# Expert tiles of a graph network with routed experts: features turned by a transposing DMA instead of TensorE

## The chip, the cores and the metric

The kernel runs on one core of a Trainium2 chip. The metric is device time in microseconds (us) of one launch. A core has five engines that each work through their own queue in order: PE (TensorE, products and transposes by a matmul with an identity), ACT (ScalarE), DVE (VectorE), POOL (GpSimd) and SP (SyncE, here only an issuer of DMAs). DMAs are issued from SP, ACT or POOL and run on 16 shared DMA engines.

## The reference

Two layers over 3327 nodes with 256 features. Each has a graph attention and a per-node network. The stage that is changed is the mixture of experts of layer 0; the rest stays as it is.

```python
# layer 0
x = x + gat(layernorm(x), adj)                  # two heads
x = x + experts(layernorm(x))
# layer 1
x = x + gat1(layernorm(x), adj)                 # one head
x = x + recurrence(layernorm(x))                # 30 steps: tanh, silu, layernorm, 256x256 product

def experts(x):                                 # 16 experts, hidden size 512
    probs = softmax(x @ gate_w + gate_b)
    top_probs, top_idx = top_k(probs, 2)        # two experts a node, weights normalized
    hidden = silu(x @ w1[e]) * (x @ w2[e])      # for every expert e
    return sum over the two experts of weight * (hidden @ w3[e])
```

## The kernel before

Nodes lie in 26 tiles of 128 rows. The stages run one after the other: projections of layer 0, attention of layer 0, experts, projections and attention of layer 1, and the recurrence. While the attention's last row groups run, the router (`route`, L510) writes the normalized rows to DRAM (`table_x`) and puts every node's two choices into lists by expert (`list_tokens`, L591, scatters from POOL).

**Tiles of the experts.** `find_tiles` (L662) cuts the lists into tiles of 128 choices of one expert and gives each a slot. It runs twice: for slots 0 to 15 (`FIRST` = 16) from the first 16 node tiles, full tiles only, and for the slots from 16 on once all nodes are listed. There are 61 slots that are always worked (`ALWAYS`), and a conditional rest up to 67. For each slot it works out the expert (`table`), the rows to gather (`which`), the rows to scatter to (`to`) and the weights of the choices. `two[:, 0, :]` (L651) holds the tile numbers by slot: here tile k of the pass is in the k-th slot of the pass.

**Weights.** Three sets of expert matrices (w1, w2, w3, 512 KB each) are held, slot s using set s % 3 (`SETS`). `weights(s)` (L788) issues three loads on SP, under a condition from the third slot on (L796): `table[1, s]` is whether the expert of slot s differs from that of slot s-3 (L720), so a load is skipped when the set already holds the right expert.

**The loop.** `work_off` (L861) runs over the slots. In iteration s it issues on POOL the gather of slot s+4 (`gathered`, L757, an indirect DMA of 128 rows into a part of `rb`, two buffers of three slots each); on PE the product with w1 (`product`, L830, L835), on ACT its silu (L881), on PE the product with w2, on DVE the product of both (L885, `pT`); then the next slot's features are turned: two PE transposes with `ident` (L826) into PSUM and a copy on ACT to `hT` (L827) (`features_first`, L822); then `results(s-1)` (L846): the product with w3 on PE (L851), the weighting on DVE (L854), and the scatter from POOL to `given` (L855); last, `weights(s+2)` on SP. `e` and `pT` come from the pool `run` with three buffers of 768 columns, of which the experts use 512.

At s = 16 whatever is left of the second `find_tiles` is flushed, and `layer1_parameters` (L359) issues six loads from ACT's queue; at s = 22 `score_vectors` (L371) does four small products on DVE. A scheduler orders the instructions of each engine by priority and by dependence, unless the kernel pins them (`keep_in_program_order`, `issue_after`, manual dependences).

**The recurrence** at the end already turns four of its seven row groups by DMA: ACT copies the float32 values as two planes of int16 halves (L1095), SP writes them to DRAM (`apart`, L1097), and SP reads them back with a transposing DMA (L1107), two tiles of 128x256 at a time.

Of the kernel before, what the change touches and what calls it, by code (L numbers as in the profile page):

```python
# [21 lines left out]
P = 128  # L22
# [5 lines left out]
MOST = 6  # L28
# [3 lines left out]
def gat_moe_gat_recurrent_ffn(ctx: ExitStack, tc: tile.TileContext, a: dict, out: bass.AP):  # L32
    nc = tc.nc
    N, D = a["x"].shape
    KD = D // P
# [6 lines left out]
    HID = a["w1"].shape[2]  # L42
    FH = HID // P
# [54 lines left out]
    ident = const.tile([P, P], F32, name="ident")  # L98
# [260 lines left out]
    def layer1_parameters():  # L359
        for dst, src in (  # L360
            (wv1[:, :, 2:], a["gW"].rearrange("(k p) c -> p k c", p=P)),
            (va.rearrange("p s d -> p (s d)"), every_partition(a["ga"], 2 * D)),
            (fW, a["fWT"].rearrange("(k p) d -> p k d", p=P)),
            (lw, a["ln_w"]),
            (lb, a["ln_b"]),
            (fb, every_partition(a["fb"], D)),
        ):
            tc.keep_in_program_order(nc.scalar.dma_start(dst, src))
        nc.vector.memset(ones_r, 1.0)

    def score_vectors():  # L371
# [10 lines left out]
    with ExitStack() as moe:  # L382
# [22 lines left out]
        ps_o = moe.enter_context(tc.tile_pool(name="ps0o", bufs=2, space=PSUM))  # L405
# [5 lines left out]
        with ExitStack() as pre:  # L411
# [58 lines left out]
            behind = None  # L470
# [9 lines left out]
            for ts in groups0[1:3]:  # L480
                behind = take_graph(ts, behind)
# [23 lines left out]
        run = moe.enter_context(tc.tile_pool(name="edge0", bufs=3))  # L505
        rows_p = moe.enter_context(tc.tile_pool(name="rows0", bufs=2))
        gate = moe.enter_context(tc.tile_pool(name="gate", bufs=1))
        turn = moe.enter_context(tc.tile_pool(name="turn", bufs=2))

        def route(ts):  # L510

            n, t0 = len(ts), ts[0]
            whole = [P, n, E]
            normalized([x[:, t, :] for t in ts], [row[:, j, :] for j in range(n)])
            here = slice(t0 * P, (t0 + n) * P)
# [6 lines left out]
            for j0 in range(0, n, 2):  # L522
                hT = turned(row[:, j0 : j0 + 2, :], turn, ps)
# [16 lines left out]
            logit, one, two, tmp = gtile("logit"), gtile("one"), gtile("two"), gtile("tmp")  # L540
# [41 lines left out]
            d, both = gcol("d"), gcol("both")  # L582
# [28 lines left out]
            if ts is groups0[3]:  # L611

                for s in range(3):
                    ahead.append(gathered(s))
            if ts is groups0[2]:
                pieces = begin_tiles()

# [27 lines left out]
        row = gate.tile([P, MOST, D], F32, name="row")  # L645
# [16 lines left out]
        def find_tiles(end, s0, n):  # L662


            here = slice(s0, s0 + n)
# [53 lines left out]
            s1 = max(s0, SETS)  # L719
# [35 lines left out]
        places = []  # L755

        def gathered(s):  # L757
            if s % 3 == 0 or s == ALWAYS:
                places.append(rows_p.tile([P, MOST * P], F32, name="rb"))
            row = places[-1][:, (s % 3) * D : (s % 3 + 1) * D]  # L760
            nc.gpsimd.indirect_dma_start(  # L761
                out=row, out_offset=None, in_=table_x[: EARLY * P, :] if s < FIRST else table_x,
                in_offset=bass.IndirectOffsetOnAxis(ap=which[:, s : s + 1], axis=0),
            )
            return row

        behind = None
        sets = [first_set]
# [53 lines left out]
        def features_first(row):  # L822
            pt = ps_o.tile([P, 512], F32, name="acc0")[:, :D].rearrange("p (k q) -> p k q", k=KD)
            hT = turn.tile([P, 2, KD, P], F32, name="hT")[:, 0]
            for k in range(KD):
                nc.tensor.transpose(pt[:, k, :], row[:, k * P : (k + 1) * P], ident)  # L826
            nc.scalar.copy(hT, pt)  # L827
            return hT

        def product(hT, w):  # L830

            p = bank().rearrange("p (f q) -> p f q", f=FH)
            for f in range(FH):
                for k in range(KD):
                    nc.tensor.matmul(  # L835
                        p[:, f, :], lhsT=w[:, k, f * P : (f + 1) * P], rhs=hT[:, k, :],
                        start=(k == 0), stop=(k == KD - 1),
                    )
            return p

        def edge(name):
            return run.tile([P, MOST * P], F32, name=name)[:, :HID].rearrange("p (f q) -> p f q", f=FH)

        ahead = deque()

        def results(s, hidT):  # L846

            w3 = ew[s % SETS][2]
            po = ps_o.tile([P, 512], F32, name="acc1")[:, :D]
            for f in range(FH):  # L850
                nc.tensor.matmul(po, lhsT=hidT[:, f, :], rhs=w3[:, f, :], start=(f == 0), stop=(f == FH - 1))  # L851
            y0 = 6 * KD * HID + s % 2 * D
            y = sets[1][:, y0 : y0 + D]
            nc.vector.tensor_scalar(y, po, weight[:, s : s + 1], None, op0=ALU.mult)  # L854
            put = nc.gpsimd.indirect_dma_start(  # L855
                out=given, out_offset=bass.IndirectOffsetOnAxis(ap=to[:, s : s + 1], axis=0), in_=y, in_offset=None
            )
            tc.declare_no_dep(put.ins, group="given", reason="no two results have the same row")
            tc.add_to_no_dep_group("given", put.ins)

        def work_off(s0, s1, aside):  # L861

            hT = features_first(ahead.popleft())
            made = None
            for s in range(s0, s1 + 1):
                if s == FIRST:
                    for _ in aside:
                        pass
                    layer1_parameters()
                if s == FIRST + 6:  # L870
                    score_vectors()
                hidT = made
                if s == 1:

                    results(0, hidT)
                if s < s1:
                    if s + 4 < s1:
                        ahead.append(gathered(s + 4))
                    pa = product(hT, ew[s % SETS][0])
                    act = edge("e")  # L880
                    nc.scalar.activation(act, pa, AF.Silu)  # L881
                    next(aside, None)
                    pb = product(hT, ew[s % SETS][1])
                    made = edge("pT")
                    nc.vector.tensor_tensor(made, act, pb, ALU.mult)  # L885
                    if s + 1 < s1:
                        hT = features_first(ahead.popleft())
# [17 lines left out]
        ahead.append(gathered(3))  # L905
        weights(1)


# [23 lines left out]
        )  # L932
        behind = None
        with tc.If(more > ALWAYS - FIRST):
            ahead.extend(gathered(s) for s in range(ALWAYS, ALWAYS + 4))
# [14 lines left out]
    with ExitStack() as st:  # L950
# [6 lines left out]
        ps_o = st.enter_context(tc.tile_pool(name="ps2o", bufs=2, space=PSUM))  # L957
# [38 lines left out]
        run = st.enter_context(tc.tile_pool(name="edge2", bufs=3))  # L996
# [26 lines left out]
    with ExitStack() as st:  # L1023
        ps_t = st.enter_context(tc.tile_pool(name="ps3t", bufs=2, space=PSUM))
        turns = cycle((ps, ps_t))
        ps_o = st.enter_context(tc.tile_pool(name="ps3o", bufs=2, space=PSUM))
# [11 lines left out]
        class Group:  # L1038
# [8 lines left out]
            def put(self, ins):  # L1047
                return tc.keep_in_program_order(ins) if self.at >= COUNT else ins
# [164 lines left out]
```

## Time and profile before

| | |
|---|---|
| median of 3 runs | 1842.49 us (1841.95 to 1842.71) |
| the profiled execution | 1841.14 us, its span 1839.4 us |
| PE busy / PEld busy | 1787.4 us (97%) / 1631.7 us (89%) |
| DVE / ACT / POOL busy | 1319.1 us (72%) / 1223.9 us (67%) / 888.4 us (48%) |
| mean granted PE clock | 0.995 |
| experts: first product, last scatter issued | 388.4 us, 741.5 us |
| PE transposes of the stage (L826) | 122, in 61 tiles |
| evictions of them on ACT (L827) | 61, 372 ns each |
| loads of weights issued (L800 to L802) | 183, 512 KB each |
| DMA transposes of the recurrence (L1107) | 236, 1241 ns to issue |
| copies into two planes (L1095) | 236, 1045 ns each |

The profiled execution is one run of its own; its span runs from the first to the last instruction. In the views, PE is the matmul, PEld the loading of its stationary operand, which overlaps it, and SPq the queue of SP. A line such as `L826 PE MATMUL acc<-ident,rb` names the line of the code, the engine, the operation, the tile written and the tiles read. In a timeline the first number is the start and the second the length, both in us; consecutive instructions of a kind are merged, with their count at the end.

### The profile page before, as it was taken

How to read it: one execution, taken by the hardware profiler on the slowest of the kernel's cores; microseconds unless marked ns; L12 is line 12 of the kernel's file. 1: busy time of each engine (PE TensorE's matmuls, PEld its weight loads, DVE VectorE, ACT ScalarE, POOL GpSimd, SP SyncE). 2: the span in 40 equal slices, each digit the busy share in tenths (PEclk: the TensorE clock that was granted, in tenths of full speed). 3: DMA queues.
4: the chain of work that ended last, by engine and by line, in shares of the span. 5: the costliest groups of instructions: out<-in, count | busy, mean ns of one | idle time of the engine just before them, and what ended most of it. 6: DMA issues, size and time to landing. Idle time of an engine off the chain costs nothing.

```text
span 1839.4 us, 32502 instructions
## 1 busy us (share of the span) xinstructions
PE 1787.4 (97%) x10980; PEld 1631.7 (89%) x10980; DVE 1319.1 (72%) x4039; ACT 1223.9 (67%) x1587; POOL 888.4 (48%) x654
## 2 busy tenths in 40 slices
PE   7999999999999999799999999999999999999997
PEld 6999999898999999688888878888888888888886
DVE  6888878853222222657677678999999999999998
ACT  2877667642111111366666579999999999999994
POOL 3010212155333332100111028988898889888984
PEclk9999999999999999899999999999999999999999
DMA  8887360258999886400000036666667666666667
GB/s 178 114 123 91 66 101 16 67 187 255 349 345 333 304 301 225 159 9 22 14 18 22 12 84 172 172 172 168 171 167 178 173 172 172 172 167 169 175 172 218
DMA packets 458610, 284.44 MB, mean 155 GB/s; under 512 B 305269, under 2 KB 418220, under 8 KB 458442
## 3 DMA queue, kind: packets, MB, share of 16 engines
q1 hardware_dynamic: 442322, 249.47, 48.4%
q0 software_dynamic: 11440, 28.09, 8.8%
q10 hardware_dynamic: 4680, 4.76, 0.8%
q8 instruction: 90, 1.47, 0.3%
q14 instruction: 78, 0.64, 0.1%
HBM read 168.19 MB, written 91.69 MB: 141 GB/s over the span
## 4 chain that ended last, share of the span: by engine, by line
PE 67%; issue 10%; DVE 6%; POOL 5%; DMA 3%; ACT 1%; another core or an unknown queue 0%; SPq 0%; POOLq 0%; DVEq 0%; ACTq 0%
PE po L1120 35%; PE acc L286 24%; PE bank L1085 4%; DVE pT L281 3%; POOL given L855 2%; POOL rb L761 2%; DMA given<-wh,to 2%; PE bank L835 1%; PE acc L163 1%; PE bank L148 1%; DMA old<-kept 1%; PE bank L526 1%; PE acc L851 1%; DMA lists<-pair,ati 0%; DVE x L1130 0%
## 5 line engine op out<-in xcount | busy, mean ns | idle before, releaser
L276 ACT ACTIVATE e<-rb,minus,full 128x384 f32<-128x384 f32 (+3 forms) x494 | 399.2, 823 | 168.6 <-DVE pT L281 150.8
L1055 POOL TENSOR_TENSOR th<-th,x 128x1024 f32<-128x1024 f32 (+1 forms) x210 | 465.0, 2214 | 94.1 <-ACT th L1052 86.4
L281 DVE SCALAR_TENSOR_TENSOR pT<-e,part,adjT 128x384 f32<-128x384 f32 (+3 forms) x494 | 383.5, 782 | 117.8 <-PE acc L286 101.9
L1120 PE MATMUL po<-wc,adjT 128*128 128x256 f32 x1888 | 422.2, 379 | 0.0
L1120 PEld LDWEIGHTS po<-wc,adjT 128*128 128x128 f32 x1888 | 356.4, 190 | 47.6 <-DVE x L1130 0.3
L1130 DVE SCALAR_TENSOR_TENSOR x<-po,rr,bb 128x256 f32<-128x256 f32 x780 | 325.1, 478 | 61.8 <-PE po L1120 61.2
L286 PE MATMUL acc<-wh,pT 128*128 128x129 f32 x2704 | 311.0, 276 | 2.3 <-DVE pT L281 2.3
L286 PEld LDWEIGHTS acc<-wh,pT 128*128 128x128 f32 x2704 | 305.5, 192 | 3.6 <-DVE pT L281 3.0
L286 PE MATMUL acc<-s_wh,pT 128*128 128x257 f32 x1352 | 295.5, 381 | 3.6 <-DVE pT L281 3.6
L286 PEld LDWEIGHTS acc<-s_wh,pT 128*128 128x128 f32 x1352 | 255.8, 190 | 42.7 <-DVE pT L281 7.0
L1120 PE MATMUL po<-wc,zT 128*128 128x256 f32 x1232 | 281.0, 379 | 0.8 <-DVE x L1130 0.8
L1064 DVE BATCH_NORM_STATS2 stats<-z 128x6 f32<-128x256 f32 x780 | 274.1, 412 | 1.4 <-ACT z L1059 1.4
L1120 PEld LDWEIGHTS po<-wc,zT 128*128 128x128 f32 x1232 | 229.2, 190 | 29.7 <-issue 1.1
L1095 ACT COPY adjT<-z 128x1024 int16<-128x1024 int16 x236 | 235.2, 1044 | 4.8 <-DVE pT L281 2.0
L121 POOL TENSOR_TENSOR rstd<-ve,neg_half 128x4 f32<-128x4 f32 (+3 forms) x28 | 32.0, 1141 | 410.4 <-DVE ve L119 312.3
L1052 ACT ACTIVATE th<-x 128x1024 f32<-128x1024 f32 (+1 forms) x210 | 209.2, 996 | 29.0 <-DVE x L1130 23.8
L1075 POOL TENSOR_TENSOR rr<-rr,neg_half 128x4 f32<-128x4 f32 (+1 forms) x210 | 206.8, 985 | 26.4 <-DVE rr L1070 26.3
L1059 ACT ACTIVATE z<-th 128x1024 f32<-128x1024 f32 (+1 forms) x210 | 207.0, 986 | 7.9 <-POOL th L1055 1.8
L885 DVE TENSOR_TENSOR pT<-e,bank 128x512 f32<-128x512 f32 x61 | 41.9, 688 | 179.7 <-PE bank L835 119.6
L881 ACT ACTIVATE e<-bank 128x512 f32<-128x512 f32 x61 | 36.4, 597 | 196.9 <-PE bank L835 117.2
L835 PEld LDWEIGHTS bank<-hT,wh 128*128 128x128 f32 x1280 | 149.6, 192 | 9.3 <-issue 4.5
L835 PE MATMUL bank<-hT,wh 128*128 128x128 f32 x1280 | 150.6, 276 | 6.5 <-ACT hT L827 2.5
(196 smaller groups left out, 1546.6 us busy)
## 6 DMA issues: line engine op xcount, KB each, us to landing
wh<-in_w_dram SPq DMA_DIRECT2D x120, 512.0 KB
apart<-adjT SPq DMA_DIRECT2D x236, 256.0 KB
first_set<-in_w_dram SPq DMA_DIRECT2D x63, 512.0 KB
in_bytes<-in_adj_dram POOLq DMA_DIRECT2D x3, 2496.0 KB
adjT<-apart SPq DMA_TRANSPOSE x236
x<-in_x_dram SPq DMA_DIRECT2D x6, 512.0 KB
kept<-x SPq DMA_DIRECT2D x8, 384.0 KB
old<-kept SPq DMA_DIRECT2D x6, 512.0 KB
```

The source lines that it names most:

```text
L276: nc.scalar.activation(e[:, : n * P], rb[:, : n * P], AF.Relu, scale=sc.full[:, j, h : h + 1], bias=sc.minus[:, j, h : h + 1],)
L281: masked = nc.vector.scalar_tensor_tensor(pT[:, : n * P], e[:, : n * P], sc.part[:, j, h : h + 1], adjT[:, j // 2, ts[0] * P : (ts[-1] + 1 ...
L286: nc.tensor.matmul(po[c], lhsT=pT[:, c * P : (c + 1) * P], rhs=wh[:, j, h, :], start=(j == 0 and c % per_bank == 0), stop=(j == NT - 1), s ...
L835: nc.tensor.matmul(p[:, f, :], lhsT=w[:, k, f * P : (f + 1) * P], rhs=hT[:, k, :], start=(k == 0), stop=(k == KD - 1),)
L1052: self.put(nc.scalar.activation(self.th, self.hs, AF.Tanh, scale=1.0 / S))
L1055: self.put(nc.gpsimd.tensor_tensor(self.th, self.th, self.hs, ALU.add))
L1059: self.put(nc.scalar.activation(self.z, self.th, AF.Silu, scale=1.0 / S))
L1064: self.put(nc.vector.bn_stats(stats[:, j, :], self.z[:, j, :]))
L1075: self.put(nc.gpsimd.tensor_tensor(r, r, neg_half[:, : self.n], ALU.pow))
L1095: self.put(nc.scalar.copy(parts[:, c : c + 2], halves[:, c : c + 2]))
L1120: nc.tensor.matmul(self.po[:, j, :], lhsT=self.zT(j, k), rhs=wc[:, k, :], start=(k == 0), stop=(k == KD - 1),)
L1130: nc.vector.scalar_tensor_tensor(self.hs[:, j, :], self.po[:, j, :], self.r[:, j : j + 1], bb, op0=ALU.mult, op1=ALU.add)
```

## The change

From slot 19 (`FIRST + 3`) to slot 60 the features are no longer turned on PE. In iteration s:

- on ACT, behind the silu of slot s, the gathered rows of slot s+4 are copied as two planes of int16 halves into the 256 columns of the `e` tile that the experts don't use (`put`), and POOL writes them to DRAM (`asked`, six buffers);
- on SP, after the results of slot s-1 and ahead of `weights(s+2)`, a transposing DMA reads slot s+2 back into `face` (three buffers) (`face`);
- `features_first(s)` then only hands over the `face` tile.

Slots before 19, and the conditional ones after 60, are turned as before. From s = 17 on the gathers run five slots ahead instead of four (two of them are issued at s = 16). PE's products of these slots are tied into the order in which they are written. `layer1_parameters` issues one load per slot from s = 16 on, and `score_vectors` stands at s = 24.

The tile numbers of the slots are laid out anew: in each pass, the slots of one lane (every third slot, the ones that share a weight set) hold consecutive tiles, first all of lane 0, then lane 1, then lane 2.

```diff
@@ layer1_parameters
             tc.keep_in_program_order(nc.scalar.dma_start(dst, src))
+            yield
@@
+        faces = moe.enter_context(tc.tile_pool(name="faces", bufs=3))
@@ tile numbers of the slots
-        numbers(two[:, 0, :], [[1, SLOTS]], 0, 0)
+        for s0, n in ((0, FIRST), (FIRST, ALWAYS - FIRST)):
+            no = 0
+            for lane in range(SETS):
+                here = two[:, 0, s0 + lane : s0 + n : SETS]
+                numbers(here, [[1, here.shape[1]]], no, 0)
+                no += here.shape[1]
+        numbers(two[:, 0, ALWAYS:], [[1, SLOTS - ALWAYS]], ALWAYS - FIRST, 0)
@@ find_tiles
-            tile_no = two[:, 0, :n]
+            tile_no = two[:, 0, here]
@@
+        def by_dma(s):
+            return FIRST + 3 <= s < ALWAYS
...
+        def put(s, room, behind):
+            planes = room.bitcast(I16)
+            with tc.issue_after(behind):
+                nc.scalar.copy(
+                    planes.rearrange("p (b d) -> p b d", b=2),
+                    gotten.pop(s).bitcast(I16).rearrange("p (d b) -> p b d", b=2),
+                )
+            put_down[s] = next(asked)
+            nc.gpsimd.dma_start(put_down[s], planes)
+
+        def face(s):
+            faces_of[s] = faces.tile([P, KD, P], F32, name="face")
+            nc.sync.dma_start(
+                faces_of[s].bitcast(I16), put_down.pop(s).rearrange("t (b d) -> (t b) d", b=2), transpose=True
+            )
+
+        def features_first(s):
+            if by_dma(s):
+                return faces_of.pop(s)
+            row = gotten.pop(s)
...
@@ work_off
+            parameters = layer1_parameters()
...
+                tied = by_dma(s)
                 if s == FIRST:
                     for _ in aside:
                         pass
-                    layer1_parameters()
-                if s == FIRST + 6:
+                if s == FIRST + 8:
                     score_vectors()
...
-                    if s + 4 < s1:
-                        ahead.append(gathered(s + 4))
+                    for q in range(s + 4 if s <= FIRST else s + 5, min(s + (5 if s < FIRST else 6), s1)):
+                        gathered(q)
                     pa = product(hT, ew[s % SETS][0])
-                    act = edge("e")
-                    nc.scalar.activation(act, pa, AF.Silu)
+                    act, room = edge("e")
+                    silu = nc.scalar.activation(act, pa, AF.Silu).ins
+                    if by_dma(s + 4):
+                        put(s + 4, room[:, HID : HID + D], silu)
+                    if FIRST <= s < ALWAYS:
+                        next(parameters, None)
                     next(aside, None)
...
                 if s > max(s0, 1):
                     results(s - 1, hidT)
+                if by_dma(s + 2):
+                    face(s + 2)
                 if s + SETS - 1 < s1:
                     weights(s + SETS - 1)
```

More of the change, by code (lines that the diff above doesn't have):

```diff
@@ L613, in route @@
                 for s in range(3):
-                    ahead.append(gathered(s))
+                    gathered(s)
             if ts is groups0[2]:
@@ L753, in find_tiles @@
             nc.vector.tensor_tensor(to[:, here], tof, spare, ALU.add)
-        places = []
+        places, asked = [], cycle([dram.tile([P, 2 * D], I16, name=f"asked{q}") for q in range(6)])
+        gotten, put_down, faces_of = {}, {}, {}
+        def by_dma(s):
+            return FIRST + 3 <= s < ALWAYS
         def gathered(s):
@@ L759, in gathered @@
                 places.append(rows_p.tile([P, MOST * P], F32, name="rb"))
-            row = places[-1][:, (s % 3) * D : (s % 3 + 1) * D]
+            rows = places[-1][:, (s % 3) * D : (s % 3 + 1) * D]
             nc.gpsimd.indirect_dma_start(
-                out=row, out_offset=None, in_=table_x[: EARLY * P, :] if s < FIRST else table_x,
+                out=rows, out_offset=None, in_=table_x[: EARLY * P, :] if s < FIRST else table_x,
                 in_offset=bass.IndirectOffsetOnAxis(ap=which[:, s : s + 1], axis=0),
             )
-            return row
+            gotten[s] = rows
+        def put(s, room, behind):
[16 more added lines that the diff above has]
+            row = gotten.pop(s)
+            pt = ps_o.tile([P, 512], F32, name="acc0")[:, :D].rearrange("p (k q) -> p k q", k=KD)
+            hT = turn.tile([P, 2, KD, P], F32, name="hT")[:, 0]
+            for k in range(KD):
+                nc.tensor.transpose(pt[:, k, :], row[:, k * P : (k + 1) * P], ident)
+            nc.scalar.copy(hT, pt)
+            return hT
         behind = None
@@ L820, in recurrence_parameters, with behind_latest @@
                 nc.vector.tensor_scalar(wc[:, k, :], wc[:, k, :], S, None, op0=ALU.mult)
[L822 to L828, printed above, removed]
+        tied, latest = False, None
+        def behind_latest(ins):
+            nonlocal latest
+            if tied and latest:
+                tc.add_manual_dep(
+                    ins.ins, latest.name,
+                    mybir.DependencyInfo(mybir.DependencyClass.NoSync, mybir.DependencyReason.DATA),
+                    reason="the experts' products in their order",
+                )
+            latest = ins.ins
         def product(hT, w):
@@ L834, in product @@
                 for k in range(KD):
-                    nc.tensor.matmul(
-                        p[:, f, :], lhsT=w[:, k, f * P : (f + 1) * P], rhs=hT[:, k, :],
-                        start=(k == 0), stop=(k == KD - 1),
+                    behind_latest(
+                        nc.tensor.matmul(
+                            p[:, f, :], lhsT=w[:, k, f * P : (f + 1) * P], rhs=hT[:, k, :],
+                            start=(k == 0), stop=(k == KD - 1),
+                        )
                     )
@@ L841, in edge @@
         def edge(name):
-            return run.tile([P, MOST * P], F32, name=name)[:, :HID].rearrange("p (f q) -> p f q", f=FH)
-        ahead = deque()
+            room = run.tile([P, MOST * P], F32, name=name)
+            return room[:, :HID].rearrange("p (f q) -> p f q", f=FH), room
         def results(s, hidT):
@@ L850, in results @@
             for f in range(FH):
-                nc.tensor.matmul(po, lhsT=hidT[:, f, :], rhs=w3[:, f, :], start=(f == 0), stop=(f == FH - 1))
+                behind_latest(
+                    nc.tensor.matmul(po, lhsT=hidT[:, f, :], rhs=w3[:, f, :], start=(f == 0), stop=(f == FH - 1))
+                )
             y0 = 6 * KD * HID + s % 2 * D
@@ L861, in work_off @@
         def work_off(s0, s1, aside):
-            hT = features_first(ahead.popleft())
+            nonlocal tied
+            parameters = layer1_parameters()
+            hT = features_first(s0)
             made = None
             for s in range(s0, s1 + 1):
+                tied = by_dma(s)
                 if s == FIRST:
@@ L876, in work_off @@
                 if s < s1:
-                    if s + 4 < s1:
-                        ahead.append(gathered(s + 4))
+                    for q in range(s + 4 if s <= FIRST else s + 5, min(s + (5 if s < FIRST else 6), s1)):
+                        gathered(q)
                     pa = product(hT, ew[s % SETS][0])
-                    act = edge("e")
-                    nc.scalar.activation(act, pa, AF.Silu)
+                    act, room = edge("e")
[4 more added lines that the diff above has]
+                        next(parameters, None)
                     next(aside, None)
                     pb = product(hT, ew[s % SETS][1])
-                    made = edge("pT")
+                    made, _ = edge("pT")
                     nc.vector.tensor_tensor(made, act, pb, ALU.mult)
                     if s + 1 < s1:
-                        hT = features_first(ahead.popleft())
+                        hT = features_first(s + 1)
                 if s > max(s0, 1):
                     results(s - 1, hidT)
+                if by_dma(s + 2):
+                    face(s + 2)
                 if s + SETS - 1 < s1:
@@ L904, in gat_moe_gat_recurrent_ffn @@
         )
-        ahead.append(gathered(3))
+        gathered(3)
         weights(1)
@@ L934, in gat_moe_gat_recurrent_ffn @@
         with tc.If(more > ALWAYS - FIRST):
-            ahead.extend(gathered(s) for s in range(ALWAYS, ALWAYS + 4))
+            for s in range(ALWAYS, ALWAYS + 5):
+                gathered(s)
             for s in range(ALWAYS, ALWAYS + SETS - 1):
```

## Prediction

> **What bounds the kernel now.** I read the page's 40 slices first (which stage is it, and what is full there), then the window table of that stage, then the timeline of a single expert tile, and last the waits of the DMA queue. Slices 9 to 16 are the expert stage (about 388 to 741 us):
>
> ```profile
> PE   7999999999999999799999999999999999999997
> ...
> DMA  8887360258999886400000036666667666666667
> ```
>
> PE and DMA are both full there, so the first question is which of them sets the pace. The window table (us, then busy time of PE, PEld, DVE, ACT, POOL, clock, DMA share, GB/s):
>
> ```profile
> 540.00:560.00 20.00, 20.00 (x157) 19.33 (x156) 4.00 (x7) 3.50 (x7) 6.82 (x7) 1.00 0.95 332
> 640.00:660.00 20.00, 20.00 (x159) 19.38 (x158) 3.90 (x7) 3.50 (x7) 6.83 (x7) 1.00 0.85 275
> 700.00:720.00 20.00, 20.00 (x157) 19.33 (x156) 4.26 (x8) 3.50 (x7) 4.89 (x5) 1.00 0.78 252
> ```
>
> The DMA share falls from 0.95 to 0.78 and PE does the same work in the same time. A stage that DMA paced would have sped up. One tile, and then the last tile, in the timeline:
>
> ```profile
> 562.22 3.76 PEld L835 LDWEIGHTS bank<-hT,wh 128*128 128x128 f32 x32
> 565.90 0.25 PEld L826 LDWEIGHTS acc<-ident,rb 128*128 128x128 f32 x2
> 566.12 1.60 PEld L851 LDWEIGHTS acc<-wh,pT 128*128 128x128 f32 x8
> 567.74 3.76 PEld L835 LDWEIGHTS bank<-hT,first_set 128*128 128x128 f32 x32
> ...
> 733.29 3.76 PEld L835 LDWEIGHTS bank<-hT,first_set 128*128 128x128 f32 x32
> 736.97 1.60 PEld L851 LDWEIGHTS acc<-wh,pT 128*128 128x128 f32 x8
> ```
>
> Differences of starts give the prices: products 565.90-562.22 = 3.68, the two transposes 0.22, the results 1.62, together 5.52 us, and no gap. (733.29-567.74)/30 = 5.518 confirms it over 30 tiles. Tile 60 has no successor to transpose, and its results start 3.68 after its products: without transposes the 0.22 is simply gone. The waits of SP say who waits for whom:
>
> ```profile
> SPq L802 <- PE acc L851: 120.9, 52, 5.3
> ```
>
> Weight loads wait for PE (a set is free only after its results), not PE for weights. PE is the bound, at 5.52 us a tile.
>
> [...]The trace has 273 ns as a record's length, but a step of 0.11 us per transpose, since records overlap; I use 0.11. [...]The last scatter (issued 741.50) releases its reader at 747.14, so up to 5.6 us here.
>
> **The change part by part.** Tiles 19 to 60 (42 of 61) lose the PE transposes. Write s for the tile whose products run.
>
> *Removed from PE:* 42 x 0.22 = 9.2 us, all of it on the path, for PE is gapless from 460 to 741 and what follows waits for the last scatter.
>
> *ACT:* a copy of 128x512 int16 (the same copy of 128x1024 takes 1.045 us at L1095, so about 0.53) replaces the eviction of 0.37. ACT is busy 3.5 of 20 us. The copy for s+4 stands behind silu(s) and waits for gather s+4; behind it on ACT is silu(s+1), due one tile later, and DVE's product needs that at the end of s+1. Cover about 3 us; beyond it the products' PSUM banks would come free late.
>
> *POOL:* one plain DMA per tile more. Not shown in this stage; from 0.57 to 0.94 us at L424, 0.97 for an indirect one. I take 0.97: 3 a tile, 2.9 plus 0.3 between each, in 5.3 us. The put waits for the ACT copy; queued behind it are the scatter of s-1 and the next gathers. The scatter has two result buffers, 10.6 us. Gathers come in threes when the last of an older three has been read; now they wait for copies four tiles ahead, instead of the transposes (40.7 us of POOL waits), so they move earlier.
>
> *SP:* one transposing DMA per tile, of half the size of L1107's: 0.62 to 1.24 us, I take 1.24. It waits for the put and for the third-last face to be used; behind it are the loads for s+2. Put(q) is issued about 3.4 us into tile q-4 and landed, with the slow 5.6, at 9; face(q) comes after the results of q-4, about 10.6 us after q-4 began, [...]with 5.6, 17.5; PE wants it at 4 x 5.3 = 21.2. [...]if the cover goes, each us late is a PE us per tile. Taken value 0, bounds 0 and +0.2 a tile (8 us); it cannot be a gain.
>
> *DMA engines.* In the last stage 236 pairs of put and transposed read (two tiles each) run in 730 us at a share of 0.67: 730 x 0.67/236 = 2.07, or 1.04 us a tile. From 470 to 735 us (48 tiles):
>
> ```profile
> q1 hardware_dynamic: 46703, 68.30, 75.8%
> q0 software_dynamic: 4387, 11.96, 12.7%
> ```
>
> 0.758 x 5.52 = 4.18 us of weights, 0.70 of gather and scatter. Added to 1.04 this is 5.92, more than a tile of 5.30. But the diff also renumbers the tiles: find_tiles' table now runs through every third slot, so one expert's tiles share a weight set and a load is skipped when the expert stays (the condition of L796). Counting the reference's routing with L662's rules: today 38 of the slots from 19 on load (slots 44, 51, 55, 59 skip; the trace has exactly four L802 issues under 0.1 us there, at 639.89, 678.52, 700.59, 722.66), afterwards 16 do. A load costs about 4.18 x 48/44 = 4.6 us, so 16/42 x 4.6 + 0.70 + 1.04 = 3.5 us of 5.30. DMA goes to a share near 0.65 and is no bound.
>
> *Before tile 19:* of slots 0 to 15, 11 load instead of 16. PE has two stalls there, 2.3 us at 435.6 with no releaser shown and 1.7 at 455.6 for a weight load. Slots 6 and 7, around the first, now skip; slot 10, the second, still loads, behind the list read of L667. Bounds -4.0 to +2 (reordering); I take -1.0.
>
> *Handover (15 to 21):* put(19) and put(20) are issued in the iteration of their own gather. The trace has gathers 18 to 20 at 478.38 to 481.9, and put(19) can't come before silu(15) at 487.2: 5 us. Gather 21 waits for the transposes of tile 17 (494.9), put(21) for silu(17) near 498.5: 3.6 us. Taken 0; upper bound one late gather, 5 us.
>
> *Moved or tied, at nothing:* parameters one per tile (ACT's six issues cost 489.2 to 492.9 in a stage where PE showed no gap); score vectors two tiles later (4 x 0.43 us of DVE, which is idle 15 of 20 us); six more IOTAs at about 20.4 us (0.2 each, before 2.5 us of POOL idleness at 21 to 23.5); the order of products is the one PE already has. The tail is unchanged.
>
> Sum against the profiled execution: 1841.1 - 9.2 - 1.0 = 1830.9 (span 1829.2). The median of the runs is 1.35 above that execution, so 1832.2.
>
> **The rivals.**
> A, *gone stalls*: both early stalls vanish with the skipped loads: 1842.5 - 9.2 - 4.0 = 1829.3. For it: fewer loads in flight. Against: the second is a queue order that remains. 0.12.
> B, *handover or late faces eat it*: 3 to 8 us given back around tiles 15 to 21 or at 0.1 to 0.2 a tile, 1835.2 to 1840.2. For it: the copies wait on gathers on an in-order engine. Against: the spare times above. 0.15.
> C, *slower, DMA becomes the bound*: if skipped loads don't take effect, a tile needs 5.92 us of DMA: 42 x (5.92-5.52) = +17, 1859. It decides from 4.6 n/42 + 1.74 = 5.52, n = 35 loads on: more than 35 of 42 is slower. For it: share 0.95 today. Against: the count of 16 and the four skips that fit. The same sign comes if the transposing reads hold up the weight packets behind them in SP's queue. 0.10.
> D, *the change doesn't do what it says*: faces are made but PE's order leaves a gap as long as the transposes, 1842. 0.05.
>
> **How the numbers follow.** Forecast 0.58, from 1830 to 1835. Under 1828 about 0.05, over 1838 about 0.15; range 1828 to 1838. What a measurement can tell from no change is about 0.2%, 3.7 us. Faster than 1838.8: 0.58 + 0.12 + 0.11 of B = 0.81; same: D and the rest of B, 0.09; slower: C, 0.10.
>
> **What would show it.** Right: L826 falls from 122 to 38 transposes; starts of L851 in steady tiles lie 5.30 apart; PE stays at 20.00 of 20 from tile 22 on; DMA share 0.5 to 0.7; some 42 transposing issues more on SP, 1.2 us each or less; L802 issues under 0.1 us become frequent. Wrong: PE waits on "face" (B, or late faces), DMA share near 1 and PE waits on weights (C), ACT idle for a gather ahead of the copy, or a step other than 5.30 with no wait shown. The forecast fails if the round trip over copy, put and read takes longer than four tiles.

## The result, and the profile after

The changed kernel takes 1834.82 us (median of 6 runs, 1833.87 to 1836.06); beside it the kernel before took 1842.48 us (6 runs, 1839.82 to 1843.16). The ratio is 0.9960, with a 95% interval of 0.9949 to 0.9970: 7.7 us faster, between 5.5 and 9.4. The forecast was 1832.2, range 1828 to 1838. The sign and the size hold; 2.6 us of the forecast gain are missing, and the experiments ask where they went. The profiled execution took 1833.87 us, its span 1832.1 (1839.4 before).

The slices of the page, in the same order as before:

```profile
PE   7999999999999999899999999999999999999998
...
DMA  8897360257696885400000037777777777777777
```

In the middle of the expert stage (slices 10 to 15) the DMA digits 8 9 9 9 8 8 of before are 7 6 9 6 8 8 now, and PE is full as before. The window table has the same columns (stretch; its length, then busy time of PE, PEld, DVE, ACT and POOL; clock; DMA share; GB/s):

```profile
540.00:560.00 20.00, 20.00 (x151) 19.17 (x151) 4.33 (x8) 4.42 (x8) 9.70 (x13) 1.00 0.60 139
640.00:660.00 20.00, 20.00 (x154) 19.25 (x153) 3.44 (x7) 4.42 (x8) 10.82 (x13) 1.00 0.81 249
700.00:720.00 20.00, 20.00 (x152) 19.17 (x151) 4.68 (x8) 3.07 (x6) 4.34 (x6) 1.00 0.84 216
```

PE is still the bound. POOL has one DMA more per tile (L788, 575 ns) and ACT's copy is longer than the eviction was (L783, 611 ns, against 372); neither is near full, POOL at 4.3 to 10.8 of 20 us and ACT at 3.1 to 4.4. In PEld's timeline a tile now has two kinds of work instead of three:

```profile
559.37 3.76 PEld L880 LDWEIGHTS bank<-face,wh 128*128 128x128 f32 x32
563.04 1.60 PEld L897 LDWEIGHTS acc<-wh,pT 128*128 128x128 f32 x8
564.67 3.42 PEld L880 LDWEIGHTS bank<-face,first_set 128*128 128x128 f32 x29
...
723.92 3.76 PEld L880 LDWEIGHTS bank<-face,first_set 128*128 128x128 f32 x32
727.60 1.60 PEld L897 LDWEIGHTS acc<-wh,pT 128*128 128x128 f32 x8
729.22 1.70 PEld L897 LDWEIGHTS acc<-first_set,pT 128*128 128x128 f32 x8
```

The products of tile 60, the last, start at 723.92 and those of the tile 30 before it at 564.67: (723.92-564.67)/30 = 5.308 us a tile, where it was 5.518. No gap stands in brackets, and no wait of PE names `face`. SP's waits show that the loads still wait for PE, as before, only in fewer cases, and that the new reads hardly wait for their puts:

```profile
SPq L842 <- PE acc L897: 64.1, 36, 5.4
...
SPq L792 <- DMA asked<-e: 0.9, 1, 0.9
```

From 470 to 735 us the queues carry:

```profile
q1 hardware_dynamic: 44288, 36.97, 49.2%
q0 software_dynamic: 6525, 17.83, 26.7%
```

q1, which holds the weights and the transposing reads, falls from 75.8 to 49.2%; q0, with gathers, puts and scatters, rises from 12.7 to 26.7%. Of the 45 issues of L842 from 484 us on, 26 took less than 0.1 us, the skipped ones; of L802's 45 before it was 4. (A skipped load leaves a record too, so the count of 183 issues stays as it was.)

**Where the 7.3 us between the two profiles came from.** The starts of PE's instructions cut each span into stages. Times in us; the last three columns are profiles of the experiments below.

| stage | before | after | e9, before again | e6, changed again | e10, none by DMA |
|---|---|---|---|---|---|
| to the first product of the experts | 388.6 | 388.4 | 389.0 | 386.4 | 386.8 |
| to the results of slot 12 | 89.3 | 89.1 | 88.4 | 87.7 | 89.0 |
| to the last result (slots 13 to 60) | 262.4 | 253.4 | 262.4 | 253.4 | 262.3 |
| to the first transposes of layer 1 (L148) | 12.3 | 13.3 | 13.0 | 12.5 | 12.6 |
| to the recurrence's first product | 338.5 | 341.0 | 340.7 | 341.4 | 338.8 |
| recurrence, to its last product | 739.2 | 738.9 | 739.0 | 738.5 | 744.5 |
| to the end | 9.1 | 8.0 | 8.5 | 8.2 | 8.5 |
| span | 1839.4 | 1832.1 | 1841.0 | 1828.1 | 1842.5 |

The stage that was changed gains 9.0 us in both profiles. 1.0 us goes before layer 1, and 2.5 us in layer 1's attention, in which no instruction was changed. There the clock shows a difference, in a stretch that PE fills either way. After:

```profile
782.00:786.00 4.00, 4.00 (x13) 3.19 (x12) 1.31 (x3) 2.54 (x5) 0.00 (x0) 0.57 0.19 49
```

and the same work before:

```profile
790.00:794.00 4.00, 4.00 (x20) 3.51 (x19) 2.11 (x4) 2.85 (x5) 0.00 (x0) 1.00 0.15 49
```

In four full us PE did 13 matmuls at a clock of 0.57, against 20 at 1.00.

### The profile page after: what moved, and what is told of

The parts are those of the page before. It is cut to its first block, busy times and chain, and to the rows that moved or that the text cites. A ratio compares the mean times of both kernels' runs of the same rounds, so it can differ in the third digit from the quotient of the medians.

```text
span 1832.1 us, 32461 instructions
## 1 busy us (share of the span) xinstructions
PE 1781.9 (97%) x10896; PEld 1626.0 (89%) x10896; DVE 1318.7 (72%) x4039; ACT 1229.3 (67%) x1587; POOL 914.2 (50%) x702
## 4 chain that ended last, share of the span: by engine, by line
PE 55%; DVE 3%; DMA 1%; issue 0%; ACT 0%; SPq 0%; POOL 0%; ACTq 0%; DVEq 0%; POOLq 0%
PE po L1176 35%; PE acc L286 15%; PE bank L1141 4%; PE acc L163 1%; DVE pT L281 1%; DMA old<-kept 0%; DVE x L1186 0%; DMA given<-wh,to 0%; PE bank L148 0%; DVE stats L1120 0%; DVE x L1194 0%; DVE low L1060 0%; SPq L1163 0%; DMA th<-given 0%; DVE high L1061 0%
## 5 line engine op out<-in xcount | busy, mean ns | idle before, releaser
L902 POOL DMA_INDIRECT given<-wh,to x61 | 61.1, 1001 | 114.4 <-DVE wh L901 99.8
L594 POOL DMA_INDIRECT lists<-pair,ati x52 | 63.5, 1222 | 109.0 <-DVE ati L581 50.8
```

## The experiments

Twelve kernels ran, in three sets, each set on a chip of its own; "before" beside them was 1837.26 us for e1 to e4, 1837.2 for e5 to e8 and 1842.65 for e9 to e12, so only ratios, or times of one set, are compared.

**e1: the new tile numbers alone**, in the kernel before.

```diff
-        numbers(two[:, 0, :], [[1, SLOTS]], 0, 0)
+        for s0, n in ((0, FIRST), (FIRST, ALWAYS - FIRST)):
...
-            tile_no = two[:, 0, :n]
+            tile_no = two[:, 0, here]
```

> The kernel before with the new tile numbers alone (a lane's slots hold consecutive tiles), turning on PE as before. My theory: PE is the bound at 5.52 us a tile, so halving the weight loads (57 to 30) gains almost nothing: 1841.5, between 1840 and 1843, L826 still 122 transposes. Rival (the fewer loads are what made the changed kernel faster): 1835.

Measured: 1837.92 us (13 runs), ratio 1.0004 (0.9995 to 1.0013). Fewer loads by themselves bring nothing, and the 1 us that the forecast put on the early slots isn't there.

**e2: the changed kernel with the old tile numbers**, so that the loads come back.

```diff
-            tile_no = two[:, 0, here]
+            tile_no = two[:, 0, :n]
```
(and the one call of `numbers` as before.)

> The changed kernel with the tile numbers of before, so 38 of the slots from 19 on load their weights instead of 16. My theory (rival C of the prediction): 4.18 + 0.70 + 1.04 = 5.9 us of DMA a tile against 5.30 of PE, so the DMA engines become the bound and the time is about 1859, PE waiting for weights or faces, DMA share near 1. Rival (DMA time is hidden anyway, as its share was 0.95 without a stall): 1835 to 1837.

Measured: 1864.88 us, ratio 1.0151 (1.0137 to 1.0166): slower than before by 28 us. The same windows and one wait of PE:

```profile
540.00:560.00 20.00, 16.84 (x122) 15.18 (x122) 4.10 (x10) 3.31 (x6) 7.85 (x10) 1.00 1.12 328
640.00:660.00 20.00, 18.39 (x131) 16.53 (x130) 4.20 (x7) 3.31 (x6) 8.25 (x10) 1.00 1.08 345
```
```profile
PE bank L874 <- DMA wh<-in_w_dram: 16.1, 14, 3.1
```

DMA is full, PE has holes, and the holes end with a weight load: here the loads set the pace. (The share adds up the times of all packets over 16 engines, and it passes 1 here: 1.12 and 1.08.) So the new numbers, useless alone, are what makes room for the faces. Whether the loads come late because the engines are full, or because transposing reads stand ahead of them in SP's queue, this run doesn't separate; the share of 1.08 to 1.12 speaks for the first.

**e3: the list read of the second `find_tiles` (L675) one step later on SP**, behind the loads of slot 10.

```diff
                 yield
+            yield
             yield from find_tiles(NT, FIRST, SLOTS - FIRST)
```

> The changed kernel with one more step ahead of the second search for tiles, so that on SP the three loads of slot 10 stand ahead of the read of the lists instead of behind it. My theory: the stall of 2.7 us ahead of slot 10 and the 3.4 us at half clock that follow it go, 3 to 4.5 us less than the changed kernel: about 1831, PE without a gap between 440 and 460 us. Rival (the stall has another cause, or the list read then comes late for slot 16): 1834 to 1837.

It aims at this line of the changed kernel (PEld, idle time in brackets):

```profile
453.52 5.28 PEld L880 LDWEIGHTS bank<-hT,wh 128*128 128x128 f32 x32 [2.69 <-issue]
```

Measured: 1830.56 us, ratio 0.9966 (0.9953 to 0.9979), where the changed kernel has 0.9960 and, as e6, 0.9971: no gain. The stall ahead of slot 10's products is gone from the timeline, and two others stand in its place, one on PE and one on DVE:

```profile
446.63 0.21 PE L688 MATMUL bank<-cnt,before 16*16 16x1 f32 x2 [3.23 <-DVE cnt L686]
```
```profile
441.96 0.48 DVE L901 TENSOR_SCALAR wh<-acc,weight 128x256 f32<-128x256 f32 x1 [7.34 <-DMA given<-wh,to]
```

DVE's weighting waits until an earlier scatter has read its buffer; that scatter stands on POOL behind the list scatters. DVE's count for the tiles stands behind the weighting, and PE behind the count. My expectation of 3 to 4.5 us fell: the wait taken away was not the last one there.

**e4: the transposing read one tile ahead of its use** instead of two.

```diff
+                    if by_dma(s + 1):
+                        face(s + 1)
                     if s + 1 < s1:
                         hT = features_first(s + 1)
...
-                if by_dma(s + 2):
-                    face(s + 2)
```

> The changed kernel with the transposing read issued one tile ahead of use instead of two. My theory: issued about 5.3 us ahead, [...]it still arrives in time: 1834.8, PE busy 20.00 of 20 us. If landing takes the 5.6 us of the prediction's upper bound, every tile waits 1.5 us: +63, 1898.

Measured: 1857.95 us, ratio 1.0111 (1.0098 to 1.0125), between the two expectations, and some 28 us above what the changed kernel's ratio gives on this chip (0.996 x 1837.26 = 1829.9): 28/42 = 0.67 us a tile on average. PE now waits for faces:

```profile
PE bank L880 <- DMA face<-asked: 6.3, 6, 2.3
```

The first two lines are of a face that came late, from its issue on SP to its use on PE, the last two of one that came in time:

```profile
601.69 1.30 SPq L792 DMA_TRANSPOSE face<-asked  x1
608.14 3.81 PE L880 MATMUL bank<-face,first_set 128*128 128x128 f32 x32 [0.52 <-DMA face<-asked]
...
590.76 1.55 SPq L792 DMA_TRANSPOSE face<-asked  x1
595.70 3.73 PE L880 MATMUL bank<-face,wh 128*128 128x128 f32 x32
```

The first took 6.4 us from the issue to the use, and one tile (5.3) doesn't cover that; the second was used 4.9 us after its issue, with no gap. What divides them are the weight loads. Of the 42 reads, 16 were issued just behind three loads that weren't skipped, and PE stood still ahead of 15 of these tiles, for 21 us in all, with 5.4 to 8.9 us from issue to use. The 26 behind skipped loads brought no gap on PE. So the loss isn't an even 0.67 us a tile: a read by itself is quick enough for one tile of lead, and a read behind weight loads isn't. (The view names the face for six of the 15 gaps, a weight load for one and nothing for eight. Two stretches of 3.41 us at half clock add to the loss.) In the changed kernel, with two tiles of lead, nothing waits. That one tile of lead is enough for every read was my estimate, which no run had shown.

**e5: TensorE kept busy ahead of layer 1** by 28 products that nobody reads, to keep the clock up.

```diff
         add_results(groups1[:3])
+        warm = ps.tile([P, 512], F32, name="bank")
+        for q in range(28):
+            tc.keep_in_program_order(
+                nc.tensor.matmul(warm[:, :P], lhsT=ident, rhs=ones_r, start=True, stop=True)
+            )
```

> The changed kernel with 28 products more on TensorE that nobody reads, between the last results of the experts and the first transposes of layer 1, where TensorE stands idle for some 7 us in both kernels and its clock is then granted at half for 10 us and again at 782 us. My theory, that the 2 us of the expert stage's gain which are missing at the end are lost to these half-clock stretches: 2 to 4 us below the changed kernel on the same chip, the stretches at 741 and 782 us gone or shorter. Rival, that the loss sits in the wait for the last scatter and the stretches are hidden: no change against the changed kernel (within 1 us), whether the stretches move or not.

Measured: 1832.27 us (13 runs), ratio 0.9975 (0.9966 to 0.9983); the changed kernel beside it, e6, 1831.17. No gain. PE's timeline:

```profile
731.78 6.41 PE L1035 MATMUL bank<-ones_r,ident 128*128 128x128 f32 x56
739.69 0.66 PE L148 MATMUL bank<-ident,x 128*128 128x128 f32 x4 [1.49 <-DVE x L1026]
744.16 1.09 PE L148 MATMUL bank<-ident,x 128*128 128x128 f32 x4 [3.81 <-DVE mv L117]
```

(Each of the 28 products leaves two records.) The gap is down from 6 or 7 us to 1.5 and 3.8, and the half-clock stretch from 10.24 to 6.83 us. But DVE sets the start of layer 1 (it adds the results as they are read), and the second stretch came all the same, at 778.39 for 3.41 us. So the half clock of the first stretch is hidden behind DVE, as the rival had it; the experiment didn't remove the second one, so it doesn't price that.

**e6: the changed kernel again.** No edit.

> The changed kernel itself, on the same chip as the other three of this set, as their measure: 0.996 of the kernel before, as in the first comparison (0.9949 to 0.997).

Measured: 1831.17 us (6 runs), ratio 0.9971 (0.9959 to 0.9983), 6 us below before.

**e7: faces only from slot 40 on**, 21 tiles.

```diff
-            return FIRST + 3 <= s < ALWAYS
+            return 40 <= s < ALWAYS
```

> The changed kernel with the features turned by DMA only from slot 40 on, 21 tiles instead of 42; slots 19 to 39 are turned on TensorE as before. My theory, that the gain is the transposes' time on TensorE, 0.22 us a tile: 21 x 0.22 = 4.6 us more than the changed kernel, about 0.9985 of the kernel before. Rival, that the gain comes from the fewer weight loads or from another place: the same time as the changed kernel, within 1 us.

Measured: 1838.40 us (21 runs), ratio 1.0013 (1.0007 to 1.0020), 7.2 us above e6 instead of 4.6. In the profile the slots behave as forecast: slots 13 to 60 take 257.8 us, 4.4 more than in e6, and the step changes at slot 40. The rest of the difference is in no slot. In the profile the recurrence took 744.0 us instead of 738.5 (below); but that execution, at 1842.52 us, is the second longest of the 21, so this stretch can't stand for the median's 2.6 us.

**e8: the changed kernel with two dead transposes of the identity per tile** where the old ones stood; nobody reads or evicts them.

```diff
             if by_dma(s):
+                pt = ps_o.tile([P, 512], F32, name="acc0")[:, :D].rearrange("p (k q) -> p k q", k=KD)
+                for k in range(KD):
+                    behind_latest(nc.tensor.transpose(pt[:, k, :], ident, ident))
                 return faces_of.pop(s)
```

> The changed kernel with two transposes of the identity on TensorE in every tile that is turned by DMA, in the place where the old ones stood, which nobody reads or copies out. My theory, that the whole gain is the time of two transposes on TensorE per tile: a step of 5.52 us instead of 5.30, 42 x 0.22 = 9.2 us more than the changed kernel, within 2 us of the kernel before or just above it. Rival, that the eviction on ScalarE or the wait for it, and not TensorE's time, was what the old transposes cost: less than 4 us more than the changed kernel.

Measured: 1839.44 us (14 runs), ratio 1.0016 (1.0008 to 1.0024), 8.3 us above e6. PEld's timeline has the old step back, with faces as operands:

```profile
562.18 3.76 PEld L883 LDWEIGHTS bank<-face,first_set 128*128 128x128 f32 x32
565.86 0.25 PEld L800 LDWEIGHTS acc<-ident 128*128 128x128 f32 x2
566.08 1.60 PEld L900 LDWEIGHTS acc<-wh,pT 128*128 128x128 f32 x8
567.70 3.76 PEld L883 LDWEIGHTS bank<-face,wh 128*128 128x128 f32 x32
```

567.70-562.18 = 5.52 us, of which 0.22 is the two dead transposes. Slots 13 to 60 take 262.4 us, as before. The gain of the stage is PE's time and nothing else: no eviction came back, and the old step did. With it given back, the kernel is 0.8 to 2.4 thousandths slower than before, so something besides the transposes costs time; the profile, of the fastest of the 14 runs, doesn't show what.

**e9: the kernel before again**, for a profile beside the next three. No edit.

> The kernel before, once more, for a profile of it on the chip of the other three of this set: a ratio of 1.000 to itself within 0.001, and an expert stage with the same 5.52 us a tile. What is asked of its profile: where its early stalls and its half-clock stretches lie here, beside the first profile of it.

Measured: 1841.81 us (13 runs), ratio 0.9997 (0.9989 to 1.0005). Its profile (table above) has the same 262.4 us for slots 13 to 60. But this time the attention took 340.7 us, and the clock was at half for 3.41 us from 790.17 on. So the stretch isn't of the change's making: the kernel before can have it too.

**e10: the changed kernel with no slot turned by DMA.**

```diff
-            return FIRST + 3 <= s < ALWAYS
+            return False
```

> The changed kernel with no slot turned by DMA: all 61 are turned on TensorE as before, while the new tile numbers, the gathers five ahead and the parameters one per tile stay. My theory now, that TensorE gives back 9.2 us and some 2 us are lost in the other parts of the change: 1.0005 to 1.0015 of the kernel before. Rival, that the 2 us are lost only with the faces (more transfers while layer 1 begins, or while the first faces are made): 1.000 or below, that is 9.2 us and not 7 to 8 us above the changed kernel.

Measured: 1846.12 us (10 runs), ratio 1.0025 (1.0016 to 1.0035), 10.3 and 10.6 us above e11 and e12. It is above the kernel before by more than I expected. Its profile, of the fastest of the ten runs, has no loss in the expert stage (262.3 us), and one of 5 us in the recurrence, as in e7. On DVE there:

```profile
1654.01 2.12 DVE L1126 TENSOR_SCALAR rr<-v 128x4 f32<-128x4 f32 x1
```

and on POOL:

```profile
1653.75 2.36 POOL L1111 TENSOR_TENSOR th<-th,x 128x1024 f32<-128x1024 f32 x1
```

The same small operation in e9, with its 170 ns, 0.65 us ahead of POOL's:

```profile
1653.80 0.17 DVE L1070 TENSOR_SCALAR rr<-v 128x4 f32<-128x4 f32 x1
```

Where it starts after POOL's long operation has begun, it ends with it (1654.01+2.12 = 1656.13, 1653.75+2.36 = 1656.11). It happens four times (1.99 to 2.12 us), with one of 0.48 us between them, and then stops.

**e11: all gathers four slots ahead**, as before.

```diff
-                    for q in range(s + 4 if s <= FIRST else s + 5, min(s + (5 if s < FIRST else 6), s1)):
+                    for q in range(s + 4, min(s + 5, s1)):
```

> The changed kernel with all gathers four slots ahead as before, so that every copy on ScalarE is asked for in the iteration of its own gather. By the spare times of the prediction ([...]the silu behind the copy is due 5.3 us after the one ahead of it, about 3 us of cover for the product that needs it): 0 to 2 us a tile late on ScalarE, so anything from no loss to 42 x 0.5 = 20 us; I expect 2 to 10 us above the changed kernel. Rival, that the fifth slot of lead does nothing for the time: within 1 us of the changed kernel, 0.9965.

Measured: 1835.86 us (5 runs), ratio 0.9964 (0.9951 to 0.9977): the same as the changed kernel, so the rival was right. The copy waited for a gather once in 42 tiles, the one of slot 21, 5.6 us after that gather's issue; in the changed kernel the same copy waits 1.8 us too:

```profile
ACT e L783 <- DMA rb<-table_x,which: 1.8, 1, 1.8
```

The gathers go out in threes when a buffer of three slots comes free (after's POOL issues them at 558.59, 559.88 and 561.16, the next three from 574.49 on), and a later place in the program doesn't change that much. My 2 to 10 us took every gather for one that was issued in its copy's own iteration.

**e12: the six parameter loads together at slot 16.**

```diff
-                    if FIRST <= s < ALWAYS:
-                        next(parameters, None)
+                    if s == FIRST:
+                        for _ in parameters:
+                            pass
```

> The changed kernel with all six parameter loads of layer 1 issued together at slot 16 as before. As predicted, spreading them costs and brings nothing: within 1 us of the changed kernel, 0.9965. Rival, that six issues in a row hold up ScalarE's queue with the copies for the first faces behind them: 1 to 4 us above the changed kernel, with a gap on TensorE near slots 17 to 20.

Measured: 1835.51 us (6 runs), ratio 0.9964 (0.9953 to 0.9976): the same as the changed kernel. As predicted, nothing.

None of the twelve is measurably faster than the changed kernel.

## Why the prediction held, and where it didn't

**The transposes, 42 x 0.22 = 9.2 us: right, and shown three ways.** Slots 13 to 60 gained 9.0 us; with 21 tiles they gained 262.4-257.8 = 4.6; with dead transposes in their place, nothing. A record of 273 ns beside a step of 110 was the trap: 42 x 2 x 0.273 = 23 us would have been the gain by the records' length.

**DMA: right in kind, too low in size.** The count of skipped loads came true (26 of 42) and kept rival C away: without it e2 is 28 us slower, where rival C had 17. The term that was too small is put and read, taken at 1.04 us a tile from a stage that moves two tiles at a time. e10 has the same tile numbers and no faces; in the window of 470 to 735 us its queues carry

```profile
q1 hardware_dynamic: 21440, 31.46, 36.9%
q0 software_dynamic: 4368, 11.93, 14.2%
```

against 49.2 and 26.7% with faces. The difference is 24.8% of 265 us, over 42 tiles 1.56 us a tile. With it a tile of e2 would need 4.18+0.70+1.56 = 6.44 us, 42 x (6.44-5.52) = 39 us more than before. Measured are 28: the share passes 1 there, so packet times added up overstate here what a tile needs.

**Face, put, copy, gather at nothing: right.** POOL took 0.58 us to issue a put where the sum had 0.97, ACT 0.61 for the copy where it had 0.53, and the one gather that came late (slot 21) left no gap on PE. The read and its landing, put at 1.24+5.6 = 6.8 us at most, with the 5.6 of the last scatter, would have left 21.2-17.5 = 3.7 us to spare. In e4 they took 4.9 us or less without weight loads ahead and 5.4 to 8.9 behind them, so this bound was too low for the worst. The changed kernel's lead of two tiles, 8.9 to 10.2 us from issue to use, was enough.

**The early slots, -1.0 us: failed.** Up to slot 12 the profiles of the kernels with the old numbers (before, e9, e2) took 89.3, 88.4 and 88.4 us, those with the new ones between 86.3 and 91.8. The first stall did shrink, as forecast (on PE):

```profile
432.33 3.62 PE L880 MATMUL bank<-hT,wh 128*128 128x128 f32 x30 [0.89 <-issue]
...
453.56 5.44 PE L880 MATMUL bank<-hT,wh 128*128 128x128 f32 x32 [2.59 <-DMA wh<-in_w_dram]
```

2.34 before became 0.89, but 1.68 became 2.59, and at the second the clock fell to half, so that the 32 products took 5.44 us instead of 3.81. e1 has this term alone: +0.0004, between -0.0005 and +0.0013. It should have been 0, with bounds on both sides. e3 adds that each stall there has another wait close behind it.

**"The tail is unchanged": failed as a statement on time.** Nobody changed its instructions, yet of 9.0 us gained in the stage 7.3 arrive. The wait from the last result to layer 1 grew from 12.3 to 13.3 us in the first pair; over all profiles it is 12.3 to 13.0 without faces (before, e1, e9, e10) and 12.5 to 13.5 with them, so that much is chance. The larger part is the half-clock stretch in layer 1's attention. Six profiles without it (before, e1, e3, e4, e8, e10) have 338.5 to 339.7 us there; seven with it have 340.7 to 341.4, and e5, which also has it, 343.1. It costs about 2 us. It was in one of four profiles without faces and in seven of ten with them. That the change makes it likelier is not shown, and the traces show something else that goes with it. In every profile all half-clock stretches start a whole number of 3.413 us apart. On this grid the attention's window with the least work on PE is, after and before:

```profile
778.99:782.41 3.41, 1.19 (x6) 0.88 (x6) 2.25 (x6) 3.08 (x8) 0.00 (x0) 1.00 0.02 4
...
785.59:789.01 3.41, 1.74 (x11) 1.27 (x9) 1.32 (x4) 2.95 (x9) 0.00 (x0) 1.00 0.02 4
```

PE was busy for 1.19 us of the one, and the stretch begins where it ends; for 1.74 of the other, and none follows. Over the fourteen profiles it is 1.19 to 1.60 us in the eight with the stretch and 1.71 to 2.02 in the six without. So in these profiles the stretch goes with where the grid lies against the work, and no run shows that the change sets that.

**The total.** At 1834.82 us the result lies at the upper edge of the band of 1830 to 1835 that the forecast held likeliest. What moved it there, early slots that gave nothing and a clock that fell in another stage, was no term of the sum, so how near the total came is in part luck.

**What stays open.** e8 and e10 are 0.8 to 3.5 thousandths above the kernel before with PE's time given back, so 1.5 to 6.4 us of loss lie outside the transposes. e1, e11 and e12 each put one part of the change aside or alone, and none shows it; the tied order of PE's products and the later score vectors were not tried alone. The half-clock stretch (2 us) and the slow stretch of the recurrence (5 us, in the profiles of e4, e7 and e10 alone) are of the right size, but a profile is one execution, and how often each occurs in the timed runs isn't known.

## What to carry to other kernels

Work taken off the full engine was worth its step there (0.11 us a transpose), not the length of its record (0.273 us), and putting dead work back in its place tests that exactly. The transposing DMA was free here only with room on the DMA engines and enough lead: the first needed weight loads to be made redundant (without that, e2 was 28 us slower than before), and the second two tiles, because a read behind weight loads took up to 8.9 us. An average over tiles (0.67 us in e4) hides that most of them lost nothing: look at which tiles wait, and at what was issued just ahead of them. Give stalls that no releaser explains no gain in a forecast, and widen the range for what can differ in stages that weren't touched: here about 2 us with a half-clock stretch, and 5 us in a slow stretch of the recurrence.

## What the runs showed of the hardware that was not expected

- TensorE's clock was granted at half in stretches of 3.41 and 10.24 us (before and after; apart from one that the end of each profile cuts off) and of 6.83 us (e5), multiples of 3.41. The 10.24 us are at layer 1's start, where PE stood idle for 6.4 us (after) and 7.0 us (before) up to the first transposes. In a profile they lie on one grid: in the changed kernel's, those at 454.73, 741.45 and 782.41 us start 84 and 12 times 3.413 us apart. PE was busy for 0.00 us in the window of 3.41 us ahead of 741.45, but for 1.17 ahead of 454.73 and 1.19 ahead of 782.41, so it wasn't always idle for the whole window. From the experts' first product to 1800 us, in all 14 profiles, a window of the grid at full clock in which PE was busy for 1.44 us or less was always followed by half clock, one with 1.74 us or more never was, and in between both occur.
- A 170 ns operation on DVE (128x4 values) took 2.0 to 2.1 us four times within 21 us of e10 when it began within a 2.36 us operation on POOL, and ended with it. This holds beyond e10: in the 14 profiles 68 such operations began with more than 0.2 us of POOL's operation left, and every one ended 23 to 31 ns after it; the 2833 that began outside took 0.15 to 0.25 us. Not every operation of DVE showed it: the four aggregates just ahead in its queue, which in e10 lay beside POOL's operations of 1653.75 (in part) and 1658.93 us, took 0.36 us there, as in e9 without it. In e4, e7 and e10 the four began 564.5 us into the recurrence, three times at the same place, and cost 5 us each time; what holds DVE's operation up isn't shown.
- A transposing read of 128 KB took SP 1.21 us to issue (L792), hardly less than one of 256 KB in the recurrence (L1107 before), 1.24 us.
